# A conv, Fourier attention and FFN block on one Trainium2 core: half of the FFN's layer norm moved to ScalarE, the first image's conv spread over other PSUM banks, and a new timetable

## The chip, the core and the metric

The kernel runs on one core of a Trainium2 chip. The core has a matrix engine (TensorE, "PE" in the profile, with its weight loads as "PEld"), a vector engine (VectorE, "DVE"), a scalar engine (ScalarE, "ACT"), GpSimd ("POOL") and a sync engine (SyncE, "SP") which here issues nearly all DMA transfers. Each engine works through its own instruction list; semaphores hold an instruction until what it reads is there and what it overwrites is no longer needed. On-chip memory is SBUF; matmuls write to PSUM, which the kernel divides into eight banks.

The metric is the device time in microseconds (us), the median of several runs. Beside it stands one execution recorded by the hardware profiler.

## What is computed

The input x has 32 images of 56 x 56 positions and 96 channels, float32. In short form, with `ln` a layer norm over channels without weights:

```python
# layer 0: layer norm, product with w_in (first half used), 3x3 conv, SiLU, residual
h = ln(x) * ln_w + ln_b
x = x + silu(conv3x3((h @ w_in + b_in)[..., :192], conv_w) + conv_b)
t = x.reshape(32, 3136, 96)
# layer 1a: Fourier attention over the 3136 tokens
h = relu(bn1(ln(t) @ w1.T))                      # 192 channels
X = fft(h, axis=tokens, norm="ortho")
xr = relu(X.real * rd - X.imag * id + rb)
xi = relu(X.imag * rd + X.real * id + ib)
t = t + bn2(ifft(xr + 1j * xi).real @ w2.T)
# layer 1b: FFN with operands rounded to 8-bit floats (5 exponent bits, 2 of
# mantissa) and results to 16 bit
h = relu(q16(q16(q8(ln(t)) @ q8(W1).T) + q8(b1)))   # 384 channels
t = t + q16(q16(q8(h) @ q8(W2).T) + q8(b2))
```

## The kernel before

**Tiling.** An image's 3136 tokens lie as 112 partitions x 28 tokens of 96 channels, in seven groups of four (112 x 4 x 96). Layer norm statistics are taken in four chunks of 8, 8, 8 and 4 tokens per partition: bn_stats and a variance on VectorE, the power -1/2 (`rs`) on POOL (line 147, names rs_a, rs_b, rs_c for the three layer norms).

**Stages of one image.** (1) `take_in` and `make_image`: chunk xl is loaded, normalized (`xa`, L409), and products with a table of rows (L165) give the image in channels, `img`. (2) The conv: a Winograd form in the row direction, three thirds r of the output channels, each as three parts of 24 matmuls (L180/184, PSUM tiles cv_b_r_part). `conv_first` and `conv_last` combine the parts on VectorE (`sd`, L193 to L201) and apply the SiLU on ScalarE (L209); `conv_tokens` transposes back to tokens (L216, tiles st_b_r_half), and `conv_end` adds to the residual tokens t (L438). (3) Forward transform: `norm_b` and `deviation` (statistics), `tokens_a` (transposes tp_n2, L158), `forth` (ph, L229, ReLU to h on ScalarE, L232), `forth_a` (first DFT factor, pa, L238); results u go to DRAM, da. (4) `fetch_a` reads them back in another order (at); `second` applies the second factor (px, L253), ScalarE and VectorE form the real and imaginary parts (av, sv, gt), `second_w2` and `second_back` multiply by w2 (pg, L292/296) and the inverse table (pe, L306); es (L308) goes to DRAM, de (L500). (5) `fetch_y` reads de back (y, L506), `back` applies the last factor (py, L314), `back_end` adds to t (L515) and, when a chunk is whole, takes the FFN's statistics st_c. (6) FFN by groups: `normal` (xn in fp8, L529, two tokens per call, all on VectorE), `ffn_start` (transposes tp_n3, L156, and their eviction n3t, L320), three times `ffn_first` (pf, L325, evicted as h1 by ScalarE, L327) and `ffn_middle` (ReLU and 8-bit cast on VectorE, L335/336), `ffn_second` (po, L342), `ffn_end` (adds, L351/352), `store` (out, L549). In the last image two of the three ReLUs are done by ScalarE (L333).

**Order.** The steps of all images are written on one timeline by `plan`: `put(when, f, ...)` notes step f of image b at `8 * b + when`; one image is 8 units. The list is sorted and emitted in that order, after which the framework's scheduler, with its own costs and priorities, sets the order on each engine; some instructions are held to program order. Stages of one image start at offsets:

```python
CONV, FIRST, BACK, FFN = -14.872, -8.324, 8.016, 10.65
```

so that about four images are in flight, and PE finds, between the steps of one image, steps of the others. SP issues loads, stores and fetches in one list. An instruction that waits holds what stands behind it on its engine.

**PSUM.** Tag "a" (two banks) holds tp_n2, tp_n3 and pf; "q" (two) holds im, cv and st; "b" (two) pa, pg, pe and po, and some weight folding at the start; "c" (two) ph, px and py.

**Start.** The weights are folded by `make_w1` (batch norm 1 into w1), `make_w2` (batch norm 2 into w2: w2x, w2y, a row in the y buffers, and the table scal) and `make_ffn` (8-bit w1q, w2q), each a list of small DVE, POOL and PE steps at a time of its own on the timeline. `ask_weights`, `ask_tables` and `ask_rest` issue their loads.

Of the kernel before, what the change touches and what calls it, by code (L numbers as in the profile page):

```python
# [38 lines left out]
F32 = mybir.dt.float32  # L39
# [46 lines left out]
def hybrid_kernel(ctx: ExitStack, tc: tile.TileContext, x, par, spar, cpar, w_in, conv_w, w1, w2, fw1, fb1, fw2, fb2, fa, fb, ib, ia, rows6, out):  # L86
# [82 lines left out]
    def conv(s, b, r, part):  # L169


        ps = s[part] = psq.tile([128, 2, 2, CT, WG], F32, tag="q", name=f"cv_{b}_{r}_{part}")
        for at, k in enumerate(PAIRS[part]):
            for dx in range(3):
                for t in range(NT):
                    cols = img[:, :, CT * t + dx : CT * (t + 1) + dx, k, :]
                    w = wv[:, k, dx, r * CB : (r + 1) * CB]
                    args = ps[t * CB : (t + 1) * CB, at], w, cols
                    if at + dx + t == 0:
                        nc.tensor.matmul(*args, start=True, stop=False)  # L180
                        continue

                    with tc.high_priority():
                        tc.keep_in_program_order(nc.tensor.matmul(*args, start=(dx == 0), stop=(dx == 2)))  # L184
        if part == 0:
            m = s["m"] = work.tile([128, 2, 2, CT, WG], F32, tag="m", name=f"m_{b}_{r}")
            nc.scalar.copy(m, s.pop(0))
# [23 lines left out]
    def to_tokens(s, b, r, half):  # L211

        g0, g1 = HALVES[half]
        pt = psq.tile([N1, g1 - g0, 128], F32, tag="q", name=f"st_{b}_{r}_{half}")
        for g in range(g0, g1):
            nc.tensor.transpose(pt[:, g - g0, :], s[:, g].rearrange("c r i h -> c (r i h)"), ident)  # L216
        return pt
# [111 lines left out]

    def ffn_relu(h1, hq, b, g, k):  # L330
        h2 = w3.tile([128, G4 * N1], F16, tag="h2", name=f"h2_{b}_{g}_{k}")
        if b == nb - 1 and k:
            nc.scalar.activation(h2, h1, AF.Relu, bias=b1q[:, k : k + 1])  # L333
        else:
            nc.vector.tensor_scalar(h2, h1, b1q[:, k : k + 1], 0.0, ALU.add, ALU.max)  # L335
        nc.vector.tensor_copy(hq[:, k, :], h2, saturate=False)  # L336

    def ffn_out(hq, b, g):
# [21 lines left out]
    class Image:  # L360


        def __init__(self, b):
# [3 lines left out]
            self.t, self.s, self.n2t, self.hq = {}, {}, {}, {}  # L367
            self.u, self.at, self.gt, self.gw, self.held = {}, {}, {}, {}, {}
            self.xa, self.xc, self.rs, self.xl, self.y, self.norm = {}, {}, {}, {}, {}, {}

        def hold(self, half):
            n = G4 * (HALVES[half][1] - HALVES[half][0])
# [147 lines left out]
    def normal(im, g, j):  # L520

        i = g // 2
        if j == 0:
            im.xc[g] = xnp.tile([N1, G4, C], F8, tag="xn", bufs=2, name=f"xn_{im.b}_{g}")
        mu, _, rs = im.norm[i]
        xc = im.xc[g]
        for j in (j, j + 1):
            at = g % 2 * G4 + j
            nc.vector.tensor_scalar(xc[:, j], im.chunk(i)[:, at, :C], mu[:, at : at + 1], rs[:, at : at + 1], ALU.subtract, ALU.mult, saturate=False)  # L529

    def ffn_start(im, g):
        im.held["n3", g] = ffn_tokens(im.xc.pop(g), im.b, g)
# [25 lines left out]
    def plan(b):  # L558
# [6 lines left out]
        CONV, FIRST, BACK, FFN = ALL  # L565
        S0, SS = 0, 2
        if nb - 4 < b < nb - 1:
            BACK, FFN = BACK + 0.762, FFN + 0.3
        if last:

            FIRST, FFN = FIRST - 0.101, FFN - 0.127
            S0 = -0.975
        back_step, ffn_step = (0.763, 0.962) if last else (0.756, 0.962)

        for i, (j0, j1) in enumerate(LN_CHUNKS):
            at = CONV - 2.503 + 0.691 * i
            ahead = 12 if b == 0 else 2.55 - 0.221 * i
            put(CONV - 7.98 + 0.01 * i if b == 1 else at - ahead, fetch, i)
            put(at - 0.55, take_in, i)
            for j in range(0, j1 - j0, 2):  # L580
                put(at + 0.066 * j, make_image, i, j)
            put(CONV + 5.858 + 1.131 * i, norm_b, i)
            put(FIRST + 2 * i - 0.477, deviation, i)
            if b:
                put(CONV - 0.456 + 0.815 * i, load, i)
        put(CONV - 0.183, make_seam)
        for r in range(NR):
            at = CONV + 1.899 * r
            for part, when in enumerate((0, 0.321, 0.817)):
                put(at + when, conv_part, r, part)  # L590
            put(at + 0.72, conv_first, r)
            put(at + 1.356, conv_last, r)
            for half in range(2):
                put(at + 1.757 + 0.239 * half, conv_tokens, r, half)
                put(at + 1.818 + 0.239 * half, conv_end, r, half)
        for g in range(NG):
            at = FIRST + g
            put(at - 0.407, tokens_a, g)
            for j2 in range(2):
                put(at + 0.065 + 0.467 * j2, forth, g, j2)  # L600
                put(at + 0.536 + 0.58 * j2, forth_a, g, j2)
            put(at + 1.249, store_a, g)
            at = BACK + back_step * g
            put(max(S0 + 4 * SS - 0.003, at - 2.9), fetch_y, g)
            put(at, back, g)
            put(at + 0.06, back_end, g)
            at = FFN + ffn_step * g
            put(at - 0.797, normal, g, 0)
            put(at - 0.375, normal, g, 2)
            put(at - 0.365, ffn_start, g)  # L610
            for k in range(3):
                put(at + 0.336 * k, ffn_first, g, k)
                put(at + 0.336 * k + 0.208, ffn_middle, g, k)
            put(at + 0.912, ffn_second, g)
            put(at + 0.997, ffn_end, g)
            put(at + 1.5, store, g)
        for g in range(NS):
            put(max(FIRST + 7.508, S0 + g - (1.4 if g % 2 else 2.2)), fetch_a, g)
        for m, (p0, p1) in enumerate(UNITS):
            both = p1 - p0 > PG  # L620
            for at, u in ((0, 0), (0.606, 1), (1.069, 2)) if both else ((0, 0), (0.674, 2)):
                at += S0 + SS * m + (0.125 if m + u == 0 else 0)
                put(at, second, m, u)
                put(at + 0.22, second_parts, m, u)
                put(at + 0.512, second_relus, m, u)
            for j0 in range(0, (p1 - p0) // 2, 2):
                at = S0 + SS * m + (2.024 if both else 1.3) - 0.017 * j0
                put(at, second_w2, m, j0)
                put(at + 0.2, second_back, m, j0)
                put(at + 0.575, store_back, m, j0)  # L630
# [1 line left out]
    def load(im, i):  # L632
        im.load(i)

    CONV, FIRST, BACK, FFN = -14.872, -8.324, 8.016, 10.65
    ALL = CONV, FIRST, BACK, FFN
    for b in range(nb):
        plan(b)
# [78 lines left out]
    def bn_fold(name, at, n):  # L717

        scale, bias = passing(f"s{name}", C, n), passing(f"o{name}", C, n)
        p = par_sb[:, at : at + 4 * n]  # L720
        nc.vector.tensor_scalar(scale, p[:, 3 * n : 4 * n], EPS, None, ALU.add)
        nc.gpsimd.tensor_tensor(scale, scale, mhalf[:C, :n], ALU.pow)
        nc.vector.tensor_tensor(scale, scale, p[:, 0:n], ALU.mult)
        nc.vector.tensor_tensor(bias, p[:, 2 * n : 3 * n], scale, ALU.mult)
        nc.vector.tensor_tensor(bias, p[:, n : 2 * n], bias, ALU.subtract)
        return scale, bias

    def bank(name):
# [28 lines left out]
    def make_w1():  # L757
# [2 lines left out]
        scale, bias = bn_fold("1", BN1, 2)  # L760
        ps = bank("w1")
        for g in range(2):
            nc.vector.tensor_scalar(w1s[:, g, :C], w1s[:, g, :C], scale[:, g : g + 1], None, ALU.mult)
            nc.vector.tensor_copy(w1s[:, g, C : C + 1], bias[:, g : g + 1])
            nc.tensor.transpose(ps[: C + 1, g * C : (g + 1) * C], w1s[:, g, :], ident[:C, :C])
        nc.vector.tensor_copy(w1a, ps[: C + 1, :H])
        ps = bank("w1c")
        nc.tensor.matmul(ps[:C, :H], centre, w1a[:C], start=True, stop=True)
        nc.vector.tensor_copy(w1a[:C], ps[:C, :H])

    def make_w2():

        w2s = raw["w2"]
        scale, bias = bn_fold("2", BN2, 1)
        nc.vector.tensor_scalar(w2s[:, :H], w2s[:, :H], scale, None, ALU.mult)
        nc.vector.tensor_copy(w2s[:, H:], w2s[:, 128:H])
        nc.gpsimd.memset(w2y, 0.0)
        ps = bank("w2")
        for g in range(2):
            nc.tensor.transpose(ps[:, g * C : (g + 1) * C], w2s[:, g * 128 : (g + 1) * 128], ident[:C, :C])  # L780
        nc.vector.tensor_copy(w2x, ps[:, :C])
        for i in range(2):
            nc.vector.tensor_copy(w2y[64 * i : 64 * i + 64, i, :], ps[64 * i : 64 * i + 64, C : 2 * C])
        ps = bank("o2")
        nc.tensor.transpose(ps[:1, :C], bias, ident[:C, :C])
        row = passing("row", 1, C)
        nc.vector.tensor_copy(row, ps[:1, :C])
        for y in ys:
            nc.sync.dma_start(y[112:113], row.unsqueeze(1).to_broadcast([1, G4, C]))
        nc.vector.tensor_scalar(scal[:, 0, :], spar_sb[:, :, RD], 2.0, None, ALU.mult)  # L790
        nc.vector.tensor_scalar(scal[:, 1, :], spar_sb[:, :, RB], 2.0, None, ALU.mult)
        nc.vector.tensor_scalar(scal[:, 2, :], spar_sb[:, :, RD], -1.0, None, ALU.mult)

    def make_ffn():

# [13 lines left out]

    for when, f in (  # L810
        (CONV + 0.01, ask_weights),
        (CONV + 1.3, make_w1),
        (CONV + 3, make_w2),
        (CONV + 6, ask_tables),
        (CONV + 9, ask_rest),
        (-2.5, make_ffn),
# [123 lines left out]
```

## Time and profile before

| | us |
|---|---|
| median of 3 runs (lowest to highest) | 3093.26 (3091.17 to 3093.85) |
| the profiled execution, its own time | 3090.75 |
| its span, first to last instruction | 3089.0 |
| TensorE busy | 3000.8 (97%) |
| VectorE busy | 2439.2 (79%) |
| ScalarE busy | 2139.5 (69%) |
| GpSimd busy | 616.7 (20%) |

The granted TensorE clock averages 0.986 of full speed. Busy times leave out waits, register and semaphore instructions and the issue of DMAs. In lines of waits, the instruction that waited stands left of the arrow and what it waited for right of it; in lines of the timeline, the first two numbers are the start and the duration, "x" counts instructions gathered into one row, and the bracket holds the idle time of the engine ahead of the row and what ended it. In lines of groups, "busy, mean ns" follow the count. Each float32 matmul of the program appears as two records.

### The profile page before, as it was taken

What the parts mean: (1) busy time and instruction counts of PE and PEld (TensorE: products, weight loads), DVE (VectorE), ACT (ScalarE), POOL (GpSimd) and SP (SyncE); (2) the same over time, 40 slices, a digit from 0 to 9 for tenths busy, and PEclk for the clock granted to TensorE, in tenths of its full rate; (3) what the DMA queues carried; (4) which work ended last, traced back from release to release, by engine and by line L of the source; (5) the groups of instructions that cost most, each with busy time, mean ns of one, the idle gap of its engine ahead of it and who ended that gap; (6) DMA issues with size and microseconds to landing.
All of it is one profiled execution on the core that took longest, in us unless ns stands there. A gap on an engine that the chain in (4) does not pass through costs nothing.

```text
span 3089.0 us, 84367 instructions
## 1 busy us (share of the span) xinstructions
PE 3000.8 (97%) x32693; PEld 2446.7 (79%) x32693; DVE 2439.2 (79%) x7554; ACT 2139.5 (69%) x5269; POOL 616.7 (20%) x398
## 2 busy tenths in 40 slices
PE   7899999999999999999999999999999999999998
PEld 5678788888788887788887888887888887788775
DVE  5548787888788888788888788888788887787778
ACT  3456667777667777677776677776677776676776
POOL 2202112222112222112221122221122221122111
PEclk9999999999999999999999999999999999999997
DMA  3532444443444443444443444444444444444442
GB/s 69 148 99 84 122 123 124 115 123 100 122 130 124 114 121 101 120 129 126 112 119 105 120 128 127 114 112 112 120 124 124 120 110 112 120 125 106 114 112 74
DMA packets 495436, 355.37 MB, mean 115 GB/s; under 512 B 329993, under 2 KB 459305, under 8 KB 494809
## 3 DMA queue, kind: packets, MB, share of 16 engines
q1 hardware_dynamic: 493146, 349.24, 42.8%
q8 instruction: 257, 4.21, 0.6%
q14 instruction: 145, 1.18, 0.1%
q10 hardware_dynamic: 1888, 0.74, 0.1%
HBM read 195.73 MB, written 154.14 MB: 113 GB/s over the span
## 4 chain that ended last, share of the span: by engine, by line
PE 88%; DMA 5%; DVE 3%; ACT 2%; issue 1%; SPq 0%; POOL 0%; DVEq 0%; ACTq 0%
PE cv L184 13%; PE ph L229 10%; PE px L253 10%; PE pa L238 9%; PE im L165 8%; PE pe L306 6%; PE pg L296 5%; PE py L314 5%; PE pg L292 5%; PE po L342 4%; PE pf L325 4%; PE cv L180 3%; PE st L216 3%; DMA de<-es 2%; PE tp_n L158 2%; DMA y<-de 2%
## 5 line engine op out<-in xcount | busy, mean ns | idle before, releaser
L184 PE MATMUL cv<-img,wv 97*32 97x196 f32 x13248 | 628.0, 332 | 0.0
L147 POOL TENSOR_TENSOR rs_c<-var_c,mhalf 112x8 f32<-112x8 f32 (+1 forms) x128 | 192.0, 1500 | 1965.0 <-DVE var_b L145 1261.4
L184 PEld LDWEIGHTS cv<-img,wv 97*32 97x32 f32 x13248 | 424.3, 109 | 112.6
L232 ACT ACTIVATE h<-ph,rs_b 112x192 f32<-112x192 f32 x896 | 338.3, 444 | 128.9 <-PE ph L229 127.9
L229 PE MATMUL ph<-w1a,n2t 97*112 97x192 f32 x1792 | 386.7, 338 | 3.3 <-DVE t L515 1.7
L253 PEld LDWEIGHTS px<-fb_sb,at 112*64 112x64 f32 (+1 forms) x3584 | 321.0, 167 | 75.9 <-issue 18.7
L238 PE MATMUL pa<-h,fa_sb 112*112 112x384 f32 x896 | 366.8, 491 | 4.9 <-DVE w1q L799 4.9
L327 ACT CAST h<-pf 128x448 f16<-128x448 f32 x672 | 364.8, 566 | 5.8 <-PE pf L325 3.0
L253 PE MATMUL px<-fb_sb,at 112*64 112x112 f32 (+3 forms) x3584 | 358.4, 274 | 7.4 <-DMA at<-da 3.8
L165 PE MATMUL im<-rows_sb,xa 112*97 112x168 f32 x1792 | 330.7, 310 | 3.1 <-DVE xa L409 1.9
L229 PEld LDWEIGHTS ph<-w1a,n2t 97*112 97x112 f32 x1792 | 273.2, 177 | 55.1 <-issue 15.9
L269 DVE SCALAR_TENSOR_TENSOR sv<-px,spar_sb,av 128x224 f32<-128x224 f32 (+2 forms) x352 | 153.9, 437 | 189.1 <-ACT av L260 188.3
L258 ACT ACTIVATE av<-px,spar_sb 128x224 f32<-128x224 f32 (+2 forms) x352 | 159.8, 454 | 200.5 <-PE px L253 199.6
L239 ACT COPY u<-pa 112x384 f32<-112x384 f32 x448 | 223.2, 498 | 102.9 <-PE pa L238 94.3
L165 PEld LDWEIGHTS im<-rows_sb,xa 112*97 112x97 f32 x1792 | 260.7, 166 | 38.5 <-issue 15.9
L147 POOL TENSOR_TENSOR rs_b<-var_b,mhalf 112x8 f32<-112x8 f32 (+1 forms) x128 | 201.8, 1578 | 425.8 <-DVE var_a L145 344.6
L336 DVE CAST hq<-h 128x448 fp8e5<-128x448 f16 x672 | 255.9, 387 | 10.2 <-ACT h L333 1.9
L335 DVE TENSOR_SCALAR h<-h,b1q 128x448 f16<-128x448 f16 x658 | 213.9, 330 | 58.9 <-ACT h L327 58.4
L141 DVE BATCH_NORM_STATS2 st_a<-xl 112x6 f32<-112x192 f32 x434 | 131.5, 353 | 154.6 <-DMA xl<-in_x 154.6
L296 PE MATMUL pg<-w2x,gt 128*112 128x96 f32 (+1 forms) x1792 | 243.5, 259 | 0.0
L529 DVE TENSOR_SCALAR xn<-t,st_c,rs_c 112x96 fp8e5<-112x96 f32 x896 | 238.5, 325 | 4.8 <-POOL rs_c L147 4.7
L296 PEld LDWEIGHTS pg<-w2x,gt 128*112 128x112 f32 (+1 forms) x1792 | 241.1, 178 | 0.0
(120 smaller groups left out, 6200.7 us busy)
## 6 DMA issues: line engine op xcount, KB each, us to landing
da<-u SPq DMA_DIRECT2D x224, 336.0 KB, 2.9
at<-da SPq DMA_DIRECT2D x224, 336.0 KB, 4.0
de<-es SPq DMA_DIRECT2D x448, 84.0 KB, 2.0
y<-de SPq DMA_DIRECT2D x224, 168.0 KB, 2.6
out<-t SPq DMA_DIRECT2D x224, 168.0 KB, 3.0
t<-in_x SPq DMA_DIRECT2D x96, 336.0 KB, 7.3
xl<-in_x SPq DMA_DIRECT2D x93, 336.0 KB, 4.1
t<-in_x SPq DMA_DIRECT2D x32, 168.0 KB, 4.3
```

The costliest lines, as they stand in the source:

```text
L147: nc.gpsimd.tensor_tensor(rs, var, mhalf[:, :n], ALU.pow)
L165: nc.tensor.matmul(ps[:, j], xa[:, j, :], rows6_sb, start=True, stop=True)
L184: tc.keep_in_program_order(nc.tensor.matmul(*args, start=(dx == 0), stop=(dx == 2)))
L229: nc.tensor.matmul(ph[:, j, :], n2t[:, 2 * j2 + j, :], w1a, start=True, stop=True)
L232: nc.scalar.activation(h[:, j], ph[:, j], AF.Relu, scale=rs[:, 2 * j2 + j : 2 * j2 + j + 1])
L238: nc.tensor.matmul(pa, fa_sb, h, start=True, stop=True)
L239: nc.scalar.copy(u[:, 2 * j2 : 2 * j2 + 2, :], pa)
L253: nc.tensor.matmul(px[rows, j], lhs, fb_sb[:, first(p) : first(p + 1)], start=True, stop=True)
L296: nc.tensor.matmul(pg[:, half, j, :], lhs, w2x, start=False, stop=True, skip_group_check=True)
L327: nc.scalar.copy(h1, pf)
L336: nc.vector.tensor_copy(hq[:, k, :], h2, saturate=False)
L529: nc.vector.tensor_scalar(xc[:, j], im.chunk(i)[:, at, :C], mu[:, at : at + 1], rs[:, at : at + 1], ALU.subtract, ALU.mult, saturate=False)
```

## The change

1. In `normal`, two of a group's four tokens are normalized on ScalarE as `Identity(scale * t + bias)`, with scale rs and a bias of -mean times rs, which one VectorE instruction per chunk makes ("shift"); the other two stay on VectorE. The last image's ReLUs all go to VectorE.
2. For image 0, conv parts 1 and 2 use the PSUM tags "c" and "b", and the transposes st use tag "a". The steps of its conv are written as an explicit list, 0.214 units apart, in which the next third's parts precede the transposes of the third before.
3. `make_w1` moves from CONV + 1.3 to CONV + 0.05 and `make_w2` from CONV + 3 to CONV + 4.3; their VectorE steps are held to program order.
4. Nearly all other times are set anew: the four offsets, the last images' corrections, and the distances within a stage.

The diff, cut to its core:

```diff
@@ def conv
-        ps = s[part] = psq.tile([128, 2, 2, CT, WG], F32, tag="q", name=f"cv_{b}_{r}_{part}")
+        pool, tag = (psum2, "cb"[part - 1]) if b == 0 and part else (psq, "q")
+        ps = s[part] = pool.tile([128, 2, 2, CT, WG], F32, tag=tag, name=f"cv_{b}_{r}_{part}")
@@ def to_tokens
-        pt = psq.tile([N1, g1 - g0, 128], F32, tag="q", name=f"st_{b}_{r}_{half}")
+        pool, tag, bufs = (psq, "q", None) if b else (psum, "a", 2)
+        pt = pool.tile([N1, g1 - g0, 128], F32, tag=tag, bufs=bufs, name=f"st_{b}_{r}_{half}")
@@ def ffn_relu
-        if b == nb - 1 and k:
-            nc.scalar.activation(h2, h1, AF.Relu, bias=b1q[:, k : k + 1])
-        else:
-            nc.vector.tensor_scalar(h2, h1, b1q[:, k : k + 1], 0.0, ALU.add, ALU.max)
+        nc.vector.tensor_scalar(h2, h1, b1q[:, k : k + 1], 0.0, ALU.add, ALU.max)
@@ def normal
+            if g % 2 == 0:
+                im.shift[i] = stp.tile([N1, mu.shape[1]], F32, tag="shift", name=f"shift_{im.b}_{i}")
+                nc.vector.scalar_tensor_tensor(im.shift[i], mu, -1.0, rs, ALU.mult, ALU.mult)
...
-            nc.vector.tensor_scalar(xc[:, j], im.chunk(i)[:, at, :C], mu[:, at : at + 1], rs[:, at : at + 1], ALU.subtract, ALU.mult, saturate=False)
+            t, scale = im.chunk(i)[:, at, :C], rs[:, at : at + 1]
+            if j < 2:
+                nc.scalar.activation(
+                    xc[:, j], t, AF.Identity, bias=im.shift[i][:, at : at + 1], scale=scale, saturate=False
+                )
+            else:
+                nc.vector.tensor_scalar(
+                    xc[:, j], t, mu[:, at : at + 1], scale, ALU.subtract, ALU.mult, saturate=False
+                )
@@ def plan
         if nb - 4 < b < nb - 1:
-            BACK, FFN = BACK + 0.762, FFN + 0.3
+            BACK, FFN = BACK + 0.4, FFN + 0.284
         if last:
-            FIRST, FFN = FIRST - 0.101, FFN - 0.127
-            S0 = -0.975
-        back_step, ffn_step = (0.763, 0.962) if last else (0.756, 0.962)
+            CONV, FIRST, FFN = CONV - 0.074, FIRST - 0.016, FFN - 0.721
+            S0, SS = -0.831, 2.033
+        back_step, ffn_step = (0.82, 0.962) if last else (0.775, 0.971)
...
-            at = CONV - 2.503 + 0.691 * i
-            ahead = 12 if b == 0 else 2.55 - 0.221 * i
+            at = CONV - 2.485 + 0.531 * i
+            ahead = 12 if b == 0 else 2.489 - 0.157 * i
...
-                put(CONV - 0.456 + 0.815 * i, load, i)
+                put(CONV - 0.346 + 0.78 * i, load, i)
...
+        if b == 0:
+            at = CONV
+            for r in range(NR + 1):
+                steps = []
+                if r < NR:
+                    steps += [(conv_part, r, 0), (conv_part, r, 1), (conv_part, r, 2), (conv_first, r)]
+                if r:
+                    steps += [(conv_tokens, r - 1, 0), (conv_end, r - 1, 0)]
+                    steps += [(conv_tokens, r - 1, 1), (conv_end, r - 1, 1)]
+                if r < NR:
+                    steps += [(conv_last, r)]
+                for f, *args in steps:
+                    put(at, f, *args)
+                    at += 0.214
...
-            put(max(S0 + 4 * SS - 0.003, at - 2.9), fetch_y, g)
+            put(max(S0 + 3 * SS + 2 - 0.003, at - 3.004), fetch_y, g)
             put(at, back, g)
-            put(at + 0.06, back_end, g)
+            put(at + 0.113, back_end, g)
             at = FFN + ffn_step * g
             put(at - 0.797, normal, g, 0)
-            put(at - 0.375, normal, g, 2)
-            put(at - 0.365, ffn_start, g)
+            put(at - 0.639, normal, g, 2)
+            put(at - 0.329, ffn_start, g)
...
-            put(at + 0.912, ffn_second, g)
-            put(at + 0.997, ffn_end, g)
-            put(at + 1.5, store, g)
+            put(at + 0.96, ffn_second, g)
+            put(at + 0.986, ffn_end, g)
+            put(at + 1.497, store, g)
...
-                at = S0 + SS * m + (2.024 if both else 1.3) - 0.017 * j0
+                at = S0 + SS * m + (2.024 if both else 1.221) + 0.062 * j0
                 put(at, second_w2, m, j0)
                 put(at + 0.2, second_back, m, j0)
                 put(at + 0.575, store_back, m, j0)
...
-    CONV, FIRST, BACK, FFN = -14.872, -8.324, 8.016, 10.65
+    CONV, FIRST, BACK, FFN = -15.042, -8.232, 8.036, 10.805
...
-        (CONV + 1.3, make_w1),
-        (CONV + 3, make_w2),
+        (CONV + 0.05, make_w1),
+        (CONV + 4.3, make_w2),
```

## Prediction

> **What bounds the kernel now.** I read the page's totals and its chain first, then the same totals cut into stretches of time, then TensorE's waits, and last the timeline around the two waits that come back.
>
> ```profile
> PE 3000.8 (97%) x32693; PEld 2446.7 (79%) x32693; DVE 2439.2 (79%) x7554; ACT 2139.5 (69%) x5269; POOL 616.7 (20%) x398
> PE 88%; DMA 5%; DVE 3%; ACT 2%; issue 1%; SPq 0%; POOL 0%; DVEq 0%; ACTq 0%
> ```
>
> TensorE (PE) is the bound, and the change leaves its matmul and transpose counts alone. So VectorE work has no direct value: only PE's waits, and matmuls at a lower clock, can be won. The table by stretches (length; busy time of PE, PEld, DVE, ACT, POOL; granted clock; DMA share; GB/s) says where they are:
>
> ```profile
> 20.00:70.00 50.00, 37.46 (x521) 25.99 (x521) 27.36 (x86) 12.25 (x24) 7.72 (x7) 0.86 0.27 64
> 400.00:2800.00 2400.00, 2372.42 (x26333) 1949.29 (x26332) 1953.67 (x6040) 1705.52 (x4214) 493.03 (x307) 1.00 0.45 118
> 3000.00:3089.00 89.00, 73.78 (x524) 53.89 (x524) 75.36 (x248) 58.54 (x131) 12.59 (x8) 0.79 0.28 72
> ```
>
> In 20 to 70 us PE idles 12.5 us and runs at 0.86 of its clock; in the middle 2400 us it idles 27.6 us; in the last 89 us it idles 15.2 us while DVE is busy 75.4. PE's waits, whole run (total, times, longest):
>
> ```profile
> PE py L314 <- DMA y<-de: 19.7, 20, 2.9
> PE st L216 <- ACT s L209: 13.9, 6, 5.7
> PE tp_n L158 <- ACT h L327: 10.7, 27, 0.6
> PE pa L238 <- DVE w1q L799: 4.9, 1, 4.9
> ```
>
> Limited to 400 to 2800 us, the first is 15.9 us in 18 waits, the third 9.6 in 25: once per image almost, 25.5 us in 25.8 images (an image takes 2400/25.8 = 93 us). The second is the first image's transposes waiting for the silu; it also drops the clock:
>
> ```profile
> 39.28 3.81 PE L184 MATMUL cv<-img,wv 97*32 97x196 f32 x43
> ...
> 48.08 1.99 PE L184 MATMUL cv<-img,wv 97*32 97x196 f32 x43
> ...
> 52.65 0.65 PE L216 MATMUL st<-ident,s 128*112 128x128 f32 x4 [2.58 <-ACT s L209]
> ```
>
> The same 43 matmuls take 3.81 us after the 5.7 us wait and 1.99 us later.
>
> **What the Trainium skill says.** "TensorE: Matmul & The Clock Gate", Part 1: after an idle window of about 3.4 us the clock falls to half, and needs about as long a busy stretch to return. The trace agrees: 3.81 against 1.99 us behind a 5.7 us wait. The same page's "Architectural detail" has ScalarE and VectorE as strict FIFOs, so an early instruction that waits holds all behind it. "DMA: Bandwidth & Descriptors", "Anatomy of one DMA": a semaphore wait of a DMA happens on the issuing sequencer; SP, which issues all DMAs here, is therefore a queue in which one late store holds a fetch. The steady timeline below shows just this.
>
> **Steady state.** One image's y fetch:
>
> ```profile
> 1431.03 0.48 ACT L308 COPY es<-pe 112x384 f32<-112x384 f32 x1
> ...
> 1432.86 2.82 SPq L549 DMA_DIRECT2D out<-t  x1
> 1435.73 1.60 SPq L500 DMA_DIRECT2D de<-es  x2
> ...
> 1436.79 1.17 DVE L141 BATCH_NORM_STATS2 st_a<-xl 112x6 f32<-112x192 f32 x4 [3.43 <-DMA xl<-in_x]
> 1440.01 0.32 SPq L549 DMA_DIRECT2D out<-t  x1
> 1440.60 4.10 SPq L506 DMA_DIRECT2D y<-de  x5
> 1443.46 0.90 PE L314 MATMUL py<-y,ia_sb 113*112 113x384 f32 x2 [0.26 <-DMA y<-de]
> ```
>
> The last es is ready at 1431.5, but its store goes out at 1435.7, 4.2 us later, because SP stands at an out<-t store, which waits for a DVE add, which stands behind layer-norm statistics that wait 3.43 us for the xl load. The y fetch follows at 1440.6, and PE meets it late.
>
> In the built instruction order of the changed kernel the es store stands ahead of both out<-t stores, and the xl load ahead of three at loads. PE's own work between the last pe and the first py becomes shorter (sum of the durations there: 12.46 before, 10.22 us after), so the deadline is earlier too. Counting from the end of pe: es +0.7; de stores issued +0.8 to +2.4 and landed by +6 (2.0 us median, page); the second out<-t ready about +5.6; y issued about +6; its first tile 2.6 to 2.9 us later, +8.9. Against +10.2 this leaves 1.3 us. I take the y wait as gone. The tp_n2 wait goes with its order: one tp_n2 instead of two directly behind the last pf, so that the shortest PE work between a "h1" eviction's matmul and the tp_n2 that reuses its bank grows from 0.76 to 1.33 us, against an eviction of 0.57.
> Upper bound: 25.5 us in the stretch.
>
> **The norm.** 896 VectorE norms become 448, plus 128 shifts; ScalarE gets 448 and loses the last image's 14 relus.
>
> ```profile
> L529 DVE TENSOR_SCALAR xn<-t,st_c,rs_c 112x96 fp8e5<-112x96 f32 x896 | 238.5, 325 | 4.8 <-POOL rs_c L147 4.7
> L259 ACT ACTIVATE av<-px,spar_sb 128x224 f32<-128x224 f32 (+2 forms) x352 | 189.6, 539 | 0.0
> ```
>
> DVE: half of 238.5 = -119; shifts 128 x 0.17 (the row of t<-var_b, same shape) = +22; relus 14 x 0.33 = +5; so 2439 - 92 = 2347 (76%). ScalarE: no row has this shape. From above, L259 (scale and bias pointers, 224 wide, 0.539 us) less 128 elements at "ScalarE: Activation LUTs" ("What ACT_TABLE_LOAD costs": 0.833 ns an element) gives 0.43 us, and that section's own price, 280 + 93 + 0.833 x 96, gives 0.45; from below, 0.36 when the 93 ns of overlap it gives for back-to-back ones applies (L259 agrees: 560 by that price, 539 measured). I take 0.41: 448 x 0.41 = 184, less 14 x 0.683 = 9.4, so 2139 + 175 = 2314 (75%). Neither engine becomes the bound. What counts is position: the four activations of two groups stand together, 1.65 us, behind a DVE shift that waits for POOL's rs_c; behind them on ScalarE stand h evictions, av and h1, and PE waits for those. PE's slack there, in sums of durations, is 2.8 to 3.9 us, so mostly hidden; I charge 0.2 us an image: 6 us. Without that cover, the whole 1.65 us, four times an image, would be 6.6 us an image. A gain from the lighter DVE is not excluded either, but no steady PE wait above names a norm: 0.
> So steady: 25.5 - 6, about **20** (5 to 35).
>
> **Start.** Image 0's conv parts 1 and 2 go to banks c and b of pools not in use yet and its transposes to bank a. In the built order six conv parts now run before the first transposes, and the last three before the second ones; so PE has work while DVE and ScalarE make the silu. Walking the chain with measured durations (conv part 2.0, sd 0.56 each, row writes, silu 0.95), the last image-0 silu's transposes start at about 47.9 instead of 62.95 (the row 62.95 is in the timeline). Taken back: seven DVE steps of make_w2 (w2x, w2y, row, scal; 0.15 to 0.26 us each, 1.4 us), moved from before the conv to behind it, and twelve statistics of 0.29 us now stand between image 0's last add and its first variance, so tp_n2_0_0 follows 8.6 us behind those transposes instead of 6.3: at about 56.5 instead of 69.2, after a 4 us PE wait which may halve the clock again. SP: the y-row stores now wait for a DVE copy at about 50 (35 before), and the table load fb behind them comes 15 us later; px needs it only beyond 120 us, and the fold's results beyond 130, so hidden. Net 12.5. The w1q wait of 4.9 (its weights no longer load behind a store of u) falls to about 2: 3; the first y wait, 2.9 with its half clock, about 2.5. Sum **18** (8 to 24).
>
> **Tail.** The last 40 us are paced by DVE, 5.0 to 5.15 us a group for 7 groups. Each group loses two norms of 0.27 (start to start), gets back a relu pair of 0.33 each (on ScalarE before): -0.5 + 0.66, about 0. The last image's new times can go both ways: **0** (-8 to +8).
>
> **Sum.** 18 + 20 + 0 = 38. The profiled execution took 3090.75 us (span 3089.0), 2.5 less than the median 3093.26. So 3052.7 profiled, and 3055.2 as a median.
>
> **The rivals.**
> - A: the start gain comes, the steady one does not: the y fetch still stands behind two out<-t stores, the deadline is 2.2 us earlier, and if DVE's add is 1.3 us later than I count, the wait is back. For: behind the de stores SP's order is the same. Against: the 4.2 us that es lost is gone. 18 + 0 = 18, plus or minus 6: 3075.
> - B: the start gain is eaten: the 4 us wait before tp_n2_0_0 halves the clock for the next 10 us and the fold comes late. 18 falls to 4; with the steady 20: 3069.
> - C, slower: ScalarE in strict order stands at the norm activations until shift and rs_c are there. POOL's rs_c takes 1.5 us and DVE is in order; if the four activations come 2 us earlier in the queue than their data, h and h1 evictions are late by 2 + 1.65 - 2.8, about 0.85 us, four times an image, 3.4 x 32 = 109 us. Against gains of 38 it ends at 3164; it decides from 38/32 = 1.2 us an image. For: two more engines between statistics and transposes. Against: the norm is placed 0.8 of a unit, 9 us, ahead of the matmuls, and DVE waited only 4.7 us in the whole run for rs_c (L529's row).
> - D: the change does not do what it says: the start wait only moves from st to tp_n2_0_0 and the new times bring as much as they cost: 3093.
>
> **How the numbers follow.** Mine 0.55, A 0.17, B 0.13, C 0.08, D 0.07. What can be told from no change is 0.2%, 6.2 us: faster means below 3087. Mine, A and B are faster (0.85), with part of D and some of C's light end: 0.87; within: 0.05; slower: C mainly, 0.08. Range: my low end, steady 35 + start 22 + tail 3 = 60, is 3033, and 3030 with some more; up, A and B with their bounds reach 3083. C and the upper half of D are left out.
>
> **What would show it.** In the profile after: image 0's last st at about 48 and tp_n2_0_0 near 56; half clock shorter in 20 to 70 (clock over 0.90, PE idle under 10 us); y<-de and tp_n<-h1 waits in the middle stretch under 8 us together, PE busy there above 2380 per 2400; es store directly behind es; an xn row on ACT at 0.36 to 0.45 us x448 and DVE near 76%, ACT near 75%. I am wrong if PE waits on ScalarE's h or h1 beyond 10 us in the middle, if the y wait keeps its size, or if the tail beyond 3000 moves by over 8 us.

## The result, and the profile after

The changed kernel takes 3037.58 us (median of 4 runs, 3036.24 to 3049.39), the kernel before 3092.22 in the runs beside it: a ratio of 0.9834, 95% interval 0.9811 to 0.9858. The forecast was 3055, with a range of 3030 to 3083. The profiled execution took 3038.6 us, its span is 3036.8; the span of before was 3089.0, so 52.2 us are to be accounted for.

The same views of the kernel after, in the order of the prediction. First the page's totals:

```profile
PE 2978.4 (98%) x32693; PEld 2445.3 (81%) x32693; DVE 2348.2 (77%) x7248; ACT 2277.4 (75%) x5703; POOL 647.5 (21%) x398
```

PE has the same 32693 records, and its busy time still fell by 22.4 us (3000.8 before). So of the 52.2 us only 29.8 are idle time that the wait views can list; the other 22.4 were inside rows that count as busy. Some 13 of these are half clock: summed over the trace's record of the granted clock, PE's busy time lost 36.7 us to it before and 24.0 after. What the other 9 to 10 are isn't shown. The stretches (length; busy time of PE, PEld, DVE, ACT, POOL; clock; DMA share; GB/s):

```profile
20.00:70.00 50.00, 44.62 (x582) 38.21 (x581) 31.49 (x101) 20.08 (x45) 12.94 (x10) 0.93 0.25 64
70.00:140.00 70.00, 62.96 (x663) 49.50 (x663) 35.14 (x105) 33.17 (x82) 15.43 (x10) 0.88 0.52 139
400.00:2800.00 2400.00, 2392.87 (x26700) 1973.48 (x26699) 1900.98 (x5857) 1847.20 (x4638) 530.39 (x312) 1.00 0.45 120
3000.00:3036.80 36.80, 25.99 (x159) 15.14 (x159) 31.82 (x108) 22.11 (x51) 6.04 (x4) 0.71 0.27 70
```

In the middle PE idles 7.1 us of 2400 (27.6 before). In 20 to 70 us it idles 5.4 (12.5 before) at a better clock; from 70 to 140 us the clock is lower than before in this execution (0.88 for 0.93). PE's waits, whole run (total, times, longest):

```profile
PE py L317 <- DMA y<-de: 10.1, 11, 3.4
PE ps_wt L701 <- DMA win<-in_w_in: 7.2, 1, 7.2
PE st L219 <- ACT s L211: 7.2, 4, 3.4
PE px L256 <- DMA at<-da: 4.0, 2, 2.6
PE tp_n L158 <- DVE t L447: 3.6, 1, 3.6
```

The wait of tp_n2 for h1 is gone, and so is that for w1q; the y wait fell to half. Between 400 and 2800 us the list is down to its first line and 0.2 us more:

```profile
PE py L317 <- DMA y<-de: 6.7, 10, 1.3
PE ph L232 <- DVE t L516: 0.2, 1, 0.2
```

The norm's new rows (busy, mean ns | idle before):

```profile
L535 ACT ACTIVATE xn<-t,shift,rs_c 112x96 fp8e5<-112x96 f32 x448 | 183.6, 484 | 22.7 <-DVE shift L529 22.7
L539 DVE TENSOR_SCALAR xn<-t,st_c,rs_c 112x96 fp8e5<-112x96 f32 x448 | 128.5, 324 | 10.3 <-PE tp_n L156 10.3
L529 DVE SCALAR_TENSOR_TENSOR shift<-st_c,rs_c 112x8 f32<-112x8 f32 (+1 forms) x128 | 20.7, 162 | 7.1 <-POOL rs_c L147 3.0
```

One ScalarE norm lasts 484 ns, but in rows of two and four they overlap: 183.6 us busy for 448 is 0.41 us each. ScalarE waits 22.7 us in the whole run for the shift.

Where the time was gained is read best from landmarks in the timeline, the start of the same PE instruction in both traces:

| first matmul of | before | after | difference |
|---|---|---|---|
| im, image 1 | 60.2 | 47.5 | -12.7 |
| im, image 3 | 194.5 | 189.3 | -5.2 |
| im, image 6 | 477.1 | 466.4 | -10.7 |
| im, image 16 | 1409.3 | 1387.6 | -21.7 |
| im, image 31 | 2806.4 | 2764.4 | -42.0 |
| end of the span | 3089.0 | 3036.8 | -52.2 |

So about 11 us by image 6 (of 13 at image 1, 7.5 are lost again, and regained), 31 in the 25 images from 6 to 31, and 10 in the tail. These are two single executions. Three of the experiments below (e8, e11, e12) have the changed kernel's instruction lists up to image 6 and show how far one execution differs from the next: their lead over before is 12.5 to 15.3 us at image 1, 8.2 to 11.0 at image 3 and 8.5 to 13.4 at image 6.

### The profile page after: what moved, and what is told of

Read it like the earlier page. It is cut to its first block, busy times and chain, and to the rows that moved or that the text cites. A ratio compares the mean times of both kernels' runs of the same rounds, so it can differ in the third digit from the quotient of the medians.

```text
span 3036.8 us, 84414 instructions
## 1 busy us (share of the span) xinstructions
PE 2978.4 (98%) x32693; PEld 2445.3 (81%) x32693; DVE 2348.2 (77%) x7248; ACT 2277.4 (75%) x5703; POOL 647.5 (21%) x398
## 4 chain that ended last, share of the span: by engine, by line
PE 88%; DMA 5%; DVE 3%; ACT 2%; issue 1%; POOL 0%; SPq 0%; ACTq 0%; DVEq 0%
PE cv L186 14%; PE ph L232 10%; PE px L256 10%; PE pa L241 9%; PE im L165 7%; PE pe L309 6%; PE pg L299 5%; PE py L317 5%; PE pg L295 5%; PE po L342 4%; PE pf L328 4%; PE cv L182 3%; PE st L219 3%; PE tp_n L158 2%; DMA de<-es 2%; DMA xl<-in_x 1%
## 5 line engine op out<-in xcount | busy, mean ns | idle before, releaser
L186 PE MATMUL cv<-img,wv 97*32 97x196 f32 x13248 | 621.6, 331 | 0.0
L147 POOL TENSOR_TENSOR rs_c<-var_c,mhalf 112x8 f32<-112x8 f32 (+1 forms) x128 | 206.7, 1615 | 1894.1 <-DVE var_c L145 879.1
L165 PE MATMUL im<-rows_sb,xa 112*97 112x168 f32 x1792 | 321.2, 313 | 2.1 <-DVE xa L410 1.4
L147 POOL TENSOR_TENSOR rs_b<-var_b,mhalf 112x8 f32<-112x8 f32 (+1 forms) x128 | 227.7, 1788 | 397.3 <-DVE var_a L145 310.2
L335 DVE TENSOR_SCALAR h<-h,b1q 128x448 f16<-128x448 f16 x672 | 220.1, 329 | 40.6 <-ACT h L330 36.1
L167 ACT COPY img<-im 97x336 f32<-97x336 f32 x448 | 205.5, 461 | 48.6 <-PE im L165 25.8
L295 PE MATMUL pg<-w2y,gt 128*112 128x192 f32 (+1 forms) x896 | 226.8, 335 | 1.1 <-DVE gt L282 0.7
```

What stands on the lines that cost most here:

```text
L147: nc.gpsimd.tensor_tensor(rs, var, mhalf[:, :n], ALU.pow)
L165: nc.tensor.matmul(ps[:, j], xa[:, j, :], rows6_sb, start=True, stop=True)
L295: nc.tensor.matmul(pg[:, :, j, :], lhs, w2y, start=True, stop=False, skip_group_check=True)
```

## The experiments

Medians are compared through their ratio to the kernel before, measured beside each of them; the changed kernel's own ratio is 0.9834. Traces are single executions.

**The start, undone and alone.** In e3 the changed kernel gets the old start:

```diff
-        pool, tag = (psum2, "cb"[part - 1]) if b == 0 and part else (psq, "q")
+        pool, tag = (psq, "q")
-        pool, tag, bufs = (psq, "q", None) if b else (psum, "a", 2)
+        pool, tag, bufs = (psq, "q", None)
-        (CONV + 0.05, make_w1),
-        (CONV + 4.3, make_w2),
+        (CONV + 1.3, make_w1),
+        (CONV + 3, make_w2),
```

with the old conv steps for image 0, unpinned folds and the old times of image 0's norm_b and deviation; e4 puts the new ones into the kernel before.

> The changed kernel with the old start: image 0's conv in the two q banks and in the old order, the two weight folds at their old times. As predicted (the new start is worth 18 us): 3052 to 3058. As the landmarks of the two traces have it (image 2's last conv matmul 5 us earlier, 11 us when image 6 begins): 3042 to 3049.

> The kernel before with the new start alone. As predicted: 3072 to 3078. As the landmarks have it: 3081 to 3088. If the start is worth nothing without the new times of image 1: 3089 to 3095.

e3: 3057.01 us (6 runs), ratio 0.9896 (0.9878 to 0.9914). e4: 3080.12 (14 runs), ratio 0.9973 (0.9959 to 0.9986). Undone, the start costs 19 us; alone, it brings about 8 (0.27%). So e3 lands where the forecast of 18 us would have it, and e4 between that and no gain. The landmarks show both as one size at first: image 6's first im is 9.1 us later in e3 than after (7 to 12 against e8, e11 and e12), and 10.0 us earlier in e4 than before. The rest of e3's 19 comes far behind the start: 12.3 us at image 31, then 6 more in the tail. The 3 us between are within what single executions do (e8, with the changed kernel's lists up to 2750 us, drifts by 6.3 us up to image 26). In the tail e3's lists differ from the changed kernel's: from 2960 us on the scheduler has set other orders on all of PE, VectorE, ScalarE and SP, though no time there was edited. So at the place of the edit the start is worth 7 to 12 us; undoing it costs more, part of it through lists 2900 us later.

**Where part of the start's gain goes in image 1.** The timelines after: PE, then DVE, then SP.

```profile
101.81 1.10 PE L219 MATMUL st<-ident,s 128*112 128x128 f32 x4 [2.88 <-ACT s L211]
...
103.18 3.81 PE L186 MATMUL cv<-img,wv 97*32 97x196 f32 x43
...
118.22 1.10 PE L219 MATMUL st<-ident,s 128*112 128x128 f32 x4 [3.39 <-ACT s L211]
```

```profile
95.21 1.15 DVE L141 BATCH_NORM_STATS2 st_a<-xl 112x6 f32<-112x192 f32 x4 [4.11 <-DMA xl<-in_x]
96.28 0.55 DVE L195 TENSOR_TENSOR sd<-m,cv 128x392 f32<-128x392 f32 x1
```

```profile
83.96 5.98 SPq L464 DMA_DIRECT2D da<-u  x2
89.99 1.27 SPq L356 DMA_DIRECT2D xl<-in_x  x2
```

Read from the bottom: SP stands at two da stores until 90 us; image 2's xl load behind them comes late; DVE waits 4.11 us for it, and image 1's conv sums sd stand behind it; the silu is late, PE waits 2.88 us, and its 43 conv matmuls run at half clock (3.81 for 2.0 us). At 118 us PE waits for a silu once more, 3.39 us, again behind image 2's statistics on DVE. e9 asks for image 2's xl loads earlier:

```diff
-            put(CONV - 7.98 + 0.01 * i if b == 1 else at - ahead, fetch, i)
+            put(CONV - 7.98 + 0.01 * i if b == 1 else at - ahead - (0.6 if b == 2 else 0), fetch, i)
```

> The changed kernel with image 2's four xl loads asked for 0.6 of a unit (7 us) earlier, so that SP issues two of them ahead of the da stores at which it stands; TensorE's list is the same. Theory X (half of the start's gain is lost again in image 1, where VectorE stands at image 2's statistics for these loads while the conv's sums and silu of image 1 stand behind them, so that PE waits for st twice, 6.3 us, and drops to half clock): the two waits st <- s shrink from 6.3 us to under 3, image 2's conv begins 3 to 5 us earlier, 3031 to 3036. Rival: the loads only land earlier and the silu is late for another reason (its own sums): 3036 to 3039.

The two waits st <- s fall from 6.3 us together (5.7 to 6.0 in e8, e11 and e12) to 3.4. e9's timelines, DVE and then PE, show that only the second one went:

```profile
89.20 1.17 DVE L141 BATCH_NORM_STATS2 st_a<-xl 112x6 f32<-112x192 f32 x4 [5.49 <-DMA xl<-in_x]
```

```profile
99.87 1.06 PE L219 MATMUL st<-ident,s 128*112 128x128 f32 x4 [2.78 <-ACT s L211]
...
101.20 3.07 PE L186 MATMUL cv<-img,wv 97*32 97x196 f32 x43
...
112.40 0.65 PE L219 MATMUL st<-ident,s 128*112 128x128 f32 x4 [0.57 <-ACT s L211]
```

For the second wait the cause is shown: with image 2's statistics earlier, 3.39 us become 0.57. The first stays (2.78 us for 2.88, and 43 matmuls in 3.07 us behind it), with VectorE standing 5.49 us for an xl load; its chain is read from the lines above and not shown by this run. Image 2's transposes st begin 8.4 us earlier than after, but 2.6 to 5.4 earlier than in e8, e11 and e12; by image 29 the lead over after is gone (0.6 us left), and the median is 3040.35 (5 runs, 3033.1 to 3049.48; ratio 0.9847, 0.9826 to 0.9868). A gain in time is not shown.

**Split and timetable apart.** e2 is the kernel before with `normal` of the changed one and nothing else new; e1 is the changed kernel with all norms on VectorE:

```diff
-            if g % 2 == 0:
+            if False:
                 im.shift[i] = stp.tile([N1, mu.shape[1]], F32, tag="shift", name=f"shift_{im.b}_{i}")
...
-            if j < 2:
+            if False:
                 nc.scalar.activation(
```

> The changed kernel with its new timetable and new start, but all norms on VectorE as before (no shift, no norm on ScalarE). Theory T (the timetable brings the steady gain: the es store ahead of the out stores on SP, and one tp_n2 behind the last pf): between 3037 and 3052, since the freed VectorE was never the bound except in the last 90 us; its tail is 3 to 6 us longer. Rival N (VectorE's lists are shorter by a tenth of a microsecond here and there, and that is what brings the xl statistics and the out adds forward): most of the steady 31 us come back, 3060 to 3075, with the y wait of before.

> The kernel before, its old timetable and old start, with half of the norms on ScalarE alone. T: 3085 to 3100, no gain that can be told, since the y fetch still stands behind the out stores. N: 3060 to 3075. A third possibility, that ScalarE's norms stand in the way of h1 and h in the old timetable: 3100 to 3130.

e1: 3154.51 us, ratio 1.0212 (1.0186 to 1.0237). e2: 3183.75, ratio 1.0302 (1.0278 to 1.0327). Neither theory had this for e1. Each half alone is a loss, of 64 us (times and start) and 93 us (split); both together gain 51. In e2, PE's waits between 400 and 2800 us, then DVE's:

```profile
PE ph L229 <- ACT h L232: 24.5, 25, 1.0
PE tp_n L158 <- ACT h L327: 21.1, 25, 1.3
PE pf L325 <- ACT h L327: 9.3, 23, 0.4
```

```profile
DVE shift L529 <- POOL rs_c L147: 81.7, 50, 1.7
```

and one place in its timeline (DVE, ScalarE, PE):

```profile
1400.69 0.16 DVE L529 SCALAR_TENSOR_TENSOR shift<-st_c,rs_c 112x8 f32<-112x8 f32 x1
1400.88 1.54 ACT L535 ACTIVATE xn<-t,shift,rs_c 112x96 fp8e5<-112x96 f32 x4 [0.62 <-DVE shift L529]
1402.33 0.70 ACT L232 ACTIVATE h<-ph,rs_b 112x192 f32<-112x192 f32 x2
1403.09 0.90 PE L229 MATMUL ph<-w1a,n2t 97*112 97x192 f32 x4 [0.98 <-ACT h L232]
```

This is the wait of the prediction's rival C: four norms stand ahead of the h evictions and PE waits a microsecond for h, once per image. PE's waits for h and h1 there come to 61.6 us (9.6 before), which is part of the 93, not all of it. The changed kernel's order keeps it away: between 400 and 2800 us its list has no such wait.

e1 and e2 share another trait: in some chunks the shift or the first norm stands directly behind var_c in VectorE's list (0 or 1 instruction between, where both kernels have 3 to 11), so that VectorE stands for POOL's power of 1.6 us. e5 and e6 pin the norms to their place in the program:

```diff
-                nc.vector.tensor_scalar(
+                tc.keep_in_program_order(nc.vector.tensor_scalar(
                     xc[:, j], t, mu[:, at : at + 1], scale, ALU.subtract, ALU.mult, saturate=False
-                )
+                ))
```

(in e5 the shift likewise).

> The kernel with only the norm split (old timetable), where the shift and VectorE's own norms are pinned to their place in the program, so that 2 us and more of other VectorE work lies between each variance var_c and the shift that needs POOL's rs_c (0.1 and 0.4 us before the pin, for two of four chunks). Theory R (what the bare split lost is VectorE standing at the shift for POOL's power, 82 us between 400 and 2800 us): that wait goes, and the time falls from 3184 to 3090 to 3115. Rival Q (the loss is ScalarE's list: four norm activations in a row ahead of the evictions h and h1): 3150 to 3190 still, with the waits ph <- h and tp_n <- h1 left at 40 us or more.

> The changed kernel with all norms on VectorE, these pinned to their place in the program: the distance between var_c and the first norm is 6 us and more in all four chunks (0 for one of them before the pin). R: the waits of VectorE on POOL's rs_c go and the time falls from 3155 to 3050 to 3090. Rival L (the load: with the norms on VectorE the adds and statistics come too late for these times): 3130 to 3170.

The wait for rs_c goes as intended (e5: 81.7 to 2.3 us; e6: 49.0 to none listed, though its wait for rs_b grows from 38.3 to 78.3), and the time rises: e5 3228.11 (ratio 1.0447, 1.0413 to 1.048), e6 3207.73 (1.0371, 1.0343 to 1.04). R, that VectorE's standing for rs_c is what the two halves lost, has fallen. New waits took over between 400 and 2800 us, first in e5, then in e6:

```profile
PE py L314 <- DMA y<-de: 30.4, 23, 1.9
PE pf L325 <- ACT n2t L222: 19.8, 25, 0.8
```

```profile
PE tp_n L156 <- DVE xn L539: 41.7, 25, 2.3
```

In e6 the pinned norms themselves are late. The rivals, ScalarE's list in e5 (Q) and VectorE's load in e6 (L), aren't shown by this either, since each pin moved other instructions too. So e10 changes a number only:

```diff
-    CONV, FIRST, BACK, FFN = -15.042, -8.232, 8.036, 10.805
+    CONV, FIRST, BACK, FFN = -15.042, -8.232, 8.036, 10.755
```

> The changed kernel with one number changed: the FFN's offset 10.755 for 10.805, 0.05 of a unit or 0.6 us earlier, for all images. If what the bare split and the bare timetable lost (93 and 64 us) is a matter of fit between times and load, so that any list that isn't set anew loses as much: 3070 to 3150. If the timetable is robust against such a shift and those losses belong to the load on VectorE and ScalarE: 3035 to 3050.

3094.94 us (22 runs), ratio 1.0015 (1.0003 to 1.0027): 0.6 us on the FFN's offset give back the whole gain. The y wait is at 24.3 us again between 400 and 2800 us, and VectorE stands 30.1 us for rs_c. The loads of VectorE and ScalarE are those of the changed kernel (2351.2 and 2276.8 us busy). So a loss of 57 us, half to two thirds of e1's and e2's, needs no change of load; the lists that the scheduler makes of the times are enough. That e1's and e2's own losses are of this kind is likely, not shown.

**The y wait.** The prediction laid it on SP's order, the es store behind the out stores. e7 pins the out stores in the kernel before, which puts the four y fetches directly behind the de stores:

```diff
-        nc.sync.dma_start(im.result[:, g * G4 : (g + 1) * G4, :], im.group(g)[:, :, :C])
+        tc.keep_in_program_order(nc.sync.dma_start(im.result[:, g * G4 : (g + 1) * G4, :], im.group(g)[:, :, :C]))
```

> The kernel before, with the out stores pinned to their place on SP alone, so that the four y fetches stand directly behind the de stores and no out store stands ahead of either. If the y wait of before is SP's order, as predicted: the wait py <- y<-de falls from 15.9 us between 400 and 2800 us to under 5, and the time by 12 to 20, to 3071 to 3079. If the wait is the shortness of time between pe and py, or another turns up in its place (the out stores late, t buffers late): 3085 to 3100.

3141.70 us, ratio 1.0158 (1.0124 to 1.0192), and the wait is longer than before, 22.6 us. SP's timeline in one image of e7:

```profile
1463.43 2.30 SPq L469 DMA_DIRECT2D at<-da  x3
1465.83 0.38 SPq L356 DMA_DIRECT2D xl<-in_x  x1
1467.41 0.93 SPq L356 DMA_DIRECT2D t<-in_x  x2
1468.43 3.55 SPq L500 DMA_DIRECT2D de<-es  x2
1475.59 2.58 SPq L506 DMA_DIRECT2D y<-de  x4
```

No out store is in the way, and y still goes out 7 us after the first de store: six loads of 336 KB stand before it, and the de stores there take 4.8 us to land (median of that window; 2.0 in the run). The kernel before has the same six in a row. The changed kernel has its xl loads ahead of the at loads, and a gap:

```profile
1407.75 2.02 SPq L470 DMA_DIRECT2D at<-da  x2
1412.80 0.93 SPq L356 DMA_DIRECT2D t<-in_x  x2
1413.82 1.08 SPq L501 DMA_DIRECT2D de<-es  x2
1415.00 1.70 SPq L561 DMA_DIRECT2D out<-t  x2
1418.61 3.71 SPq L507 DMA_DIRECT2D y<-de  x5
```

Its 336 KB t loads land in 4.1 us (median between 400 and 2800 us), 7.5 before. Since e7's other lists moved too, e12 tests the bunch with the lists of VectorE and ScalarE kept (PE's has a few instructions of each image in other places): one copy of 672 KB per image, as the profile counts it, ahead of the third at load.

```diff
+    def extra(im):
+        jk = dram.tile([N1, 16, C], F32, tag="jk", name=f"jk_{im.b}")
+        tc.keep_in_program_order(nc.sync.dma_start(jk, im.tokens[:, 0:16, :]))
+                if m == 3 and 2 < b < 29:
+                    put(at + 0.5, extra)
```

> The changed kernel with one more transfer for each of images 3 to 28: 16 tokens of x per partition (688 KB) copied to DRAM where nothing reads them, asked for by SP ahead of the third at load before the es store; all lists of PE, VectorE and ScalarE are the same. Theory B (the y wait is set by the bunch of large loads in the DMA engines ahead of the es store as much as by SP's order): de <- es lands 2 to 4 us later there, the wait py <- y<-de rises from 6.7 us to 30 or more between 400 and 2800 us, and the time by 25 to 75, to 3062 to 3112. Theory O (SP's order alone): the wait stays under 12 us and the time within 6, 3034 to 3044.

```profile
PE py L317 <- DMA y<-de: 41.1, 26, 3.8
```

3109.03 us, ratio 1.0073 (1.0054 to 1.0093). The wait is there in every image, six times its 6.7 us, and the kernel is some 72 us slower than without the copy: theory B. So what lies in the DMA engines ahead of the es store can set when y is fetched; an order on SP is only one way to get there. It isn't where the change's own gain lies, though. In the timelines of images 5 to 26 (medians, counted from the end of the last pe) the first es store goes out at 4.3 us before and at 2.4 after, and the first y fetch at 9.7 and 7.6. So 1.9 of the 2.1 us by which y comes earlier stand at the es store, which no longer has an out store ahead of it. From the first es store to y it is 5.4 us before and 5.1 after; in e7 it is about 8, in e12 about 7.

**The tail.** e8 gives the last three images the old times (offsets, S0, steps); e11 moves the norms of the last two images back to VectorE:

```diff
-            if j < 2:
+            if j < 2 and im.b < nb - 2:
```

> The changed kernel with the old times of the last three images (offsets, S0, steps), all else as changed. If the last 10 us of the gain come from the new times of the last images: 3044 to 3052. If they come from the lighter VectorE there (28 norms of images 30 and 31 moved) or from what reaches the tail earlier: 3036 to 3041.

> The changed kernel with the norms of the last two images alone back on VectorE (all lists before them as they were). If the lighter VectorE is part of the last 100 us' gain of 10 us: 28 norms of 0.27 us less 8 shifts come back, 5 to 6 us, 3041 to 3045. As I predicted (the tail comes out even): 3036 to 3039.

e8: 3042.23 us, ratio 0.9838 (0.981 to 0.9866), not to be told from 0.9834; in its trace the tail from image 26's im on is 4.8 us longer than after. e11: 3049.56, ratio 0.9872 (0.9855 to 0.9889), 12 us slower by the medians; in its trace the stretch from image 30's first im is 8.2 us longer (image 30: -0.9 us against after, the end: +7.3). e9, measured beside e11 and with nearly the changed kernel's tail, has a median of 3040.35, 9 us less. In e11's tail PE waits 6.2 us for VectorE's hq, 0.8 after. So a lighter VectorE in the last two images is worth about 8, if load and order are taken together: the other instructions there changed places too, and e3, with its norms on ScalarE but other lists in the tail, is 5.7 us longer on the same stretch. That the new times bring anything there is not shown: against e8's 4.8 stand 1.9 us in e9, which has them.

## Why the prediction was right, point by point

- **The sum and the sign** held: 38 us forecast, 52 in the profiled spans and 55 in the medians. Its terms fit less well: the start came out smaller than forecast at the place of the edit, the steady stretch and the tail larger, and these misses partly cancel. That is luck.
- **The terms as separate ones.** The prediction gave the whole steady gain of 25.5 us to the times, and to the split a cost of 6 us and a gain of nothing ("no steady PE wait above names a norm: 0"). By that account the new times without the split, e1, would be some 6 us faster than the changed kernel. They are 117 us slower, and slower than the kernel before. This step failed: the new times gain only with the norms where they now are.
- **Start, 18.** Measured 7 to 12 by the landmarks at image 6, 8 alone (e4), 19 when undone (e3, part of it in the tail). Image 0 came out as worked out: its last transposes began near 50 us, tp_n2_0_0 at 58.5 (56.5 forecast; 55.8 to 56.5 in e4, e8, e9 and e11, where the conv began 0.4 to 1.7 us earlier than before, not 1.5 later as here) after a wait of 3.6 us (4 forecast), 10.8 us earlier than before. The w1q wait is gone. The step that failed is the one that carried this gain past image 1: it took the net 12.5 as kept and looked for lost clock at tp_n2_0_0. Some 4 us (7.5 in the profiled execution) were lost between images 1 and 3, where PE waits twice for image 1's silu.
- **Steady, 20 of at most 25.5.** Measured 31 in the profiled pair; over the same 18 images (10 to 28) 21.5 after, and 16.5 to 20.5 in e8, e3 and e11 with nearly the same lists. The two waits fell by 18.8 us of their 25.5. The step "I take the y wait as gone" was too good: in the median of images 5 to 26 the first es store went out 2.4 us after pe, not 0.8 (SP stood at the t loads), the first y fetch at 7.6, not 6, and it landed at 10.3, not 8.9, where PE's own work ends at 10.1. So the wait still stands, at 6.7 us. The ceiling, read from the list of waits, was too low: PE's busy time fell as well.
- **SP's order as the cause of the y wait** holds for this change: y comes 2.1 us earlier, 1.9 of them at the es store. As a rule it doesn't hold: in e7 no out store stands ahead of the es store, and y still goes out 9.6 us after pe, as before (9.7). The large loads ahead of the store, which the prediction named only as a place in the order (the xl load ahead of the at loads), had no price in it; e12 shows that they have one.
- **The norm.** DVE 2347 forecast, 2348.2 measured. ScalarE 2314 forecast, 2277.4 measured; the norms' own 184 us came out at 183.6, but 38 of them overlap with the rows of other kinds beside them on ScalarE, which the sum left out. That neither engine becomes the bound held. The charge of 6 us for late evictions wasn't needed: no such wait is listed between 400 and 2800 us after.
- **Tail, 0.** Measured 10. The step that failed counted the norms of the last image against its ReLUs and left out image 30's, which run in the same DVE-paced stretch; e11 puts about 8 us on the two images, load and order together.
- **Rival C** (ScalarE stuck in order) was priced at 109 us for norms placed too early. The changed kernel doesn't show it; the bare split, e2, loses 93 us, and these waits are the largest on PE's list there.

The prediction took the Trainium skill's statement on the clock ("TensorE: Matmul & The Clock Gate", Part 1: half clock after an idle window of about 3.4 us, full clock after about as long a busy one) as agreeing with the trace. It agrees in kind only. In image 1 after, PE's matmuls run at half clock (3.81 us for 2.0) behind a wait of 2.88 us, shorter than the page's window; behind one of 2.58 us before, at 52.65, they didn't (2.01 us at 53.43). And the way back to full clock took PE some 10 us of busy time before (from 37.9 to 48), not 3.4. The measurements decide.

What stays open is which of e1's moved instructions account for its 117 us. Its listed waits (y 25.4, im <- xa 10.2, po <- hq 5.2 us between 400 and 2800) explain less than half, and the one repair tried made it worse.

## What to carry to other kernels

Where one engine is busy 97% of the time and all lists come from one timetable, a split of work and the times are one change: measured apart here they were +93 and +64 us, together -51, so neither is to be judged alone, and a shift of 0.6 us in one offset cost the whole gain. Behind a late small transfer, look for the large ones ahead of it in the DMA engines as well as for its place in the issuing queue. The list of waits was not the ceiling of what could be won here: compare the busy time of the bounding engine as well, and its clock. And before a few microseconds between two traces are explained, see how far two executions of the same lists differ: here up to 7 us at one landmark.

## What the runs showed of the hardware

Four ScalarE activations in a row (112 x 96, scale and bias from pointers, fp8 out) take 1.54 us (median of such rows in the changed kernel), though each lasts 484 ns: they start some 0.35 us apart. A store of 84 KB behind six loads of 336 KB lands in 4.8 us in e7, instead of 2.0. TensorE's clock fell to half during a wait of 2.88 us, and not during one of 2.58. A power on GpSimd over 112 x 8 numbers took 1.6 us, a VectorE operation of that size (the shift) 0.16.
